# Gates of the last two layers: when they are stored, how their loads are buffered, and where their reciprocal stands

## The chip, the cores and the metric

The kernel runs on one core of a Trainium2 chip, as one launch. The time is what the device needs for one execution, in microseconds (us). Five engines run side by side, each through its own list of instructions in order: TensorE (PE) multiplies, VectorE (DVE), ScalarE (ACT) and GpSimd (POOL) do elementwise work, and SyncE (SP) here only issues transfers. An instruction that waits for a semaphore holds up all that stand behind it in the list of its engine; that holds for SP's list of transfers too.

## The reference, cut to what is computed

The model has two layers on x of 4 sequences with 512 tokens of 512 channels: a state-space block, a mixture of 8 experts (top 2), causal attention with 16 heads in 4 groups, and a gated feed-forward block. In front of each of the four blocks stands the same gate, computed from a second input f (used both as k and as v) and a condition:

```
def gate(r, k, v, w, u, time_emb):                # r = x, k = v = f
    tf = sigmoid(sum(time_emb, -1))
    decay = exp(-exp(w)) * (0.5 + 0.5 * tf)
    ek  = exp(minimum(k, 30));  ekv = ek * v
    nf, df = scan forward  of (a = a * decay + ekv, b = b * decay + ek)
    nb, db = scan backward of the same
    euk = exp(minimum(u + k, 30))
    num = nf + nb - ekv + euk * v
    den = df + db - ek + euk
    return sigmoid(r) * (num / maximum(den, 1e-8)) * (0.8 + 0.2 * tf)

x = x + mamba(gate0(x, f, f));  x = x + experts(gate1(x, f, f))
x = x + attention(gate2(x, f, f));  x = x + ffn(gate3(x, f, f))
```

All of the gate except sigmoid(r) depends on f and the condition alone, so it can be made long before x of its layer is known. ek and ekv are the same in all four layers.

## The kernel before

Everything is float32, in tiles of 128 partitions (channels) by 512 tokens. PE's work runs in stages: the state-space block, the experts, attention, the feed-forward block. The gates are made beside them, in the background.

**A pair.** `gate_pair(l, b, c0)` (L220) makes two 128-channel chunks of the gate of layer l and sequence b. It is a generator: its code is cut into steps by `yield True`, and inside a step `yield False` marks finer places to stop. In the text the steps are called S0 to S6:

- S0 `keys(0)`: on SP's list, the loads of f (tile `kt`, L239), of exp(k) (`ek`, L246) and of exp(k) k (`ekv`, L248) for the first chunk.
- S1: DVE's forward scan of the first chunk's numerator (L258, reads `ekv`), and `keys(1)`, the same three loads for the second chunk.
- S2: the backward scan (L264), then the forward scan of the second numerator.
- S3: its backward scan, and the forward scan of the first denominator (reads `ek`).
- S4: its backward scan, `own(0)` (three DVE operations, L275 to L279, that add the token's own term and read `kt`), the forward scan of the second denominator.
- S5: its backward scan, `own(1)`, and in the same step the reciprocal of both denominators on ACT (L315 and two more: relu, logarithm, exponential, each on 128x1024).
- S6: three DVE operations on 128x1024 (L321, L325, L330), and the store of the finished pair to `gts[l][b]` in HBM by SP (L332).

`kt`, `ek` and `num` have two buffers, everything else one. So the load of `ekv` for the second chunk, issued in S1, writes the buffer that S1's forward scan reads.

**The order.** `make_gates` (L341) strings the pairs together: the steps of one pair follow each other, S6 of a pair is done in the same step as S2 of the next one, and S0 of the next one in the same step as S5. A pair thus takes five steps. `pump(n)` (L371) runs n steps; `nudge` (L376) runs only to the next `yield` of either kind; `have(gate)` (L389) pumps until a gate is made.

**Layers 2 and 3** have 16 pairs, made from one generator during the experts and attention. During the experts, `more` (L1494) calls one `moe.round()` after another. A round of the experts is one block of 128 tokens: PE transposes and multiplies (`pg` L793, `pn` L804, `po` L826), and SP issues weight loads for a later block: two halves of w1 (L726, 1 MB each) with their bias (L731, 512 KB), w2 (L737, 1 MB) with its bias (L738). Two sets of weight tiles alternate between blocks, and each load carries a condition that leaves it out where the set already has the right expert. Behind each of 28 rounds stand one or two steps of the gates:

```
                moe.round()
                if moe.i < ALWAYS - NT + 1:
                    with after(nc.vector):
                        pump(1 + moe.i % 2)
```

`after` holds what is traced in it behind the last DVE instruction traced so far, on DVE alone; the places on SP's and ACT's lists are the scheduler's, which mostly keeps the order of the program. SP's list therefore holds, in turn, the weights of a round and the loads and the store of gate steps.

In attention, `scores` (L1598) calls `nudge` once for each of 4 query tiles of 64 heads, 256 times in all. The gate of layer 2 for sequence b+1 is asked for at the third head of sequence b in the first group (L1687), the gates of layer 3 in the feed-forward block.

Of the kernel before, what the change touches and what calls it, by code (L numbers as in the profile page):

```python
# [19 lines left out]
NC = C // P  # L20
# [62 lines left out]
def block_kernel(ctx: ExitStack, tc: tile.TileContext, a: dict, out: bass.AP):  # L83
    nc = tc.nc
# [129 lines left out]
    gts = [[dr.tile([P, NC, T], F32, name=f"g{l}_{b}") for b in range(B)] for l in range(4)]  # L214
# [5 lines left out]
    def gate_pair(l, b, c0, dst=None, tiles=None):  # L220


        many = {"kt": 2, "ek": 2, "num": 2}

        def tile_(tag, n=1):
            if tiles is not None and tag in tiles:
                return tiles[tag]()
            shape = [P, T] if n == 1 else [P, n, T]
            return gate_pool[0].tile(shape, F32, tag=tag, name=tag, bufs=many.get(tag, 1))

        flat = lambda t: t.rearrange("p i t -> p (i t)")
        d1 = [decay[:, l * NC + c0 + i, b : b + 1] for i in range(2)]
        fl = [fall[:, l * NC + c0 + i, b : b + 1] for i in range(2)]
        kt, ek, ekv, eu = {}, {}, {}, {}

        def keys(i):
            cc = c0 + i
            kt[i] = tile_("kt")
            nc.sync.dma_start(out=kt[i], in_=a["fT"][cc * P : (cc + 1) * P, b, :])  # L239
            ek[i] = tile_("ek")  # L240
            if l == 0:
                nc.vector.tensor_scalar(ek[i], kt[i], 30.0, None, ALU.min)
                act(ek[i], ek[i], AF.Exp)
                nc.sync.dma_start(out=eks[b][:, cc, :], in_=ek[i])
            else:
                nc.sync.dma_start(out=ek[i], in_=eks[b][:, cc, :])  # L246
                ekv[i] = tile_("ekv")
                nc.sync.dma_start(out=ekv[i], in_=ekvs[b][:, cc, :])  # L248

        def products(i):  # L250
            if l == 0:
                ekv[i] = tile_("ekv")
                nc.vector.tensor_tensor(ekv[i], ek[i], kt[i], ALU.mult)
                nc.sync.dma_start(out=ekvs[b][:, c0 + i, :], in_=ekv[i])


        def forward(i, e, s):
            nc.vector.tensor_tensor_scan(s, d1[i].to_broadcast([P, T]), e, 0.0, ALU.mult, ALU.add)  # L258
            f = tile_("f")
            nc.scalar.mul(f[:, : T - 1], s[:, : T - 1], fl[i])  # L260
            return f

        def backward(i, f, s):
            nc.vector.tensor_tensor_scan(  # L264
                s[:, : T - 1][:, ::-1], d1[i].to_broadcast([P, T - 1]), f[:, : T - 1][:, ::-1],
                s[:, T - 1 : T], ALU.mult, ALU.add,
            )

        def bonus(i):

            eu[i] = tile_("eu")
            act(eu[i], kt[i], AF.Exp, bias=col("wkv_u", l * NC + c0 + i))

        def own(i):
            nc.vector.scalar_tensor_tensor(den[:, i, :], eu[i], E30, den[:, i, :], ALU.min, ALU.add)  # L275
            yield False
            nc.vector.scalar_tensor_tensor(eu[i], eu[i], E30, kt[i], ALU.min, ALU.mult)
            yield False
            nc.vector.tensor_tensor(num[:, i, :], num[:, i, :], eu[i], ALU.add)  # L279
            yield False  # L280

        keys(0)
        yield True
        num = tile_("num", 2)
        products(0)
        f = forward(0, ekv[0], num[:, 0, :])
        keys(1)
        yield True
        backward(0, f, num[:, 0, :])
        yield False  # L290
        products(1)
        f = forward(1, ekv[1], num[:, 1, :])
        yield True
        backward(1, f, num[:, 1, :])
        yield False
        den = tile_("den", 2)
        f = forward(0, ek[0], den[:, 0, :])
        yield False
        bonus(0)
        yield True  # L300
        backward(0, f, den[:, 0, :])
        yield False
        yield from own(0)
        f = forward(1, ek[1], den[:, 1, :])
        yield False
        bonus(1)
        yield True
        backward(1, f, den[:, 1, :])
        yield False
        yield from own(1)  # L310
        if tiles is not None:
            yield True

        r = tile_("rec", 2)
        nc.scalar.activation(flat(r), flat(den), AF.Relu, bias=tiny[:, 1:2])  # L315
        yield False
        act(flat(r), flat(r), AF.Ln, bias=tiny[:, 0:1])
        yield False
        act(flat(r), flat(r), AF.Exp, scale=-1.0)
        yield True  # L320
        nc.vector.scalar_tensor_tensor(  # L321
            flat(den), flat(den), DEN_MIN, flat(r), ALU.max, ALU.mult
        )
        yield False
        nc.vector.scalar_tensor_tensor(  # L325
            flat(num), flat(num), tf_out[:, b : b + 1], flat(r), ALU.mult, ALU.mult
        )
        yield False
        g = num if dst is None else dst[:, c0 : c0 + 2, :]
        nc.vector.scalar_tensor_tensor(g, den, 2.0, num, ALU.subtract, ALU.mult)  # L330
        if dst is None:
            nc.sync.dma_start(out=gts[l][b][:, c0 : c0 + 2, :], in_=g)  # L332
        yield True

    def step(pair):
        for done in pair:
            if done:
                return
            yield False

    def make_gates(which):  # L341


        pairs = [(gate_pair(l, b, c0), (l, b), c0) for l, b in which for c0 in range(0, NC, 2)]
        yield from step(pairs[0][0])
        for n, (pair, _, _) in enumerate(pairs):
            yield True
            yield from step(pair)
            yield True
            yield from step(pair)  # L350
            if n:
                old, lb, c0 = pairs[n - 1]
                yield from step(old)
                made.update([lb] * (c0 + 2 == NC))
            yield True
            yield from step(pair)
            yield True
            yield from step(pair)
            yield True
            yield from step(pair)  # L360
            if n + 1 < len(pairs):
                yield from step(pairs[n + 1][0])
        yield True
        old, lb, c0 = pairs[-1]
        yield from step(old)
        made.add(lb)

    made = set()
    making = make_gates(((0, 1), (1, 0), (0, 2), (1, 1), (0, 3), (1, 2), (1, 3)))

    def pump(n=1, until=None):  # L371
        for _ in range(n):
            while until not in made and not next(making, True):
                pass

    def nudge():  # L376
        next(making, None)

    def apply_gate(g, xs):

# [8 lines left out]
    def have(gate):  # L389
        while gate not in made:  # L390
            pump()

    def gated(l, b, xb, pool, part=slice(0, T), **kw):
        have((l, b))
# [484 lines left out]
    with ExitStack() as ph:  # L879
# [41 lines left out]
        pairs = [gate_pair(0, 0, c0, first, lent[c0 // 2]) for c0 in range(0, NC, 2)]  # L921
# [388 lines left out]
        old = None  # L1310
# [178 lines left out]
    with tc.tile_pool(name="moe_w2", bufs=1, reuse_waits="tile") as wm:  # L1489
        moe.add_slot(wm)  # L1490
        for b in range(B):
            nc.sync.dma_start(out=x[b], in_=xs_d[b])

        def more(limit):  # L1494
            while moe.i < min(limit, moe.known):
                moe.round()
                if moe.i < ALWAYS - NT + 1:
                    with after(nc.vector):
                        pump(1 + moe.i % 2)

        more(moe.i + 1)
        next(routing)
        more(moe.i + 1)
        next(routing)
        more(moe.i + 1)
        order_blocks(NEARLY, NBLK)
        moe.know(ALWAYS)
        more(NBLK - 8)
        first_group = load_group(0)

        more(NEARLY + FIRST + 2)
        results = {t: load_results(0, t, nc.gpsimd) for t in range(2)}
        more(moe.i + 1)
        for t in range(NT):
            moe.round()
            with after(nc.tensor, nc.vector, nc.scalar):
                add_results(0, t, results.pop(t))
            if t + 2 < NT:
                results[t + 2] = load_results(0, t + 2, nc.gpsimd)
        assert moe.i == ALWAYS + 2  # L1520
        early_h = gated(2, 0, x[0], wa, tag="wq", name="h2_0")
        used = nc.values_load(in_use[0:1, 0:1], min_val=0, max_val=NBLK)
        with tc.If(used > ALWAYS - NEARLY):
            moe.i = ALWAYS
            moe.know(NBLK)
            for _ in range(4):
                moe.round()
# [5 lines left out]
    with att as ph:  # L1533
# [163 lines left out]
        dense(held[0])  # L1697
        for _ in making:
            pass
        act.use(act.SILU)  # L1700


# [113 lines left out]
```

## Time and profile before

| what | value |
|---|---|
| three runs, us | 2550.01, 2553.25, 2553.5 (median 2553.25) |
| the profiled execution: time, span, us | 2547.61, 2545.9 |
| busy share of the span: PE, DVE, ACT, POOL | 95%, 55%, 40%, 11% |
| mean granted TensorE clock | 0.984 |
| experts: first and last `pg` block, us from the start | 661.4 to 1125.7 |
| attention: first `pk` to last `pd`, us | 1143.6 to about 2085 |
| feed-forward block | about 2085 to the end |
| last gate store (L332), us | 1779.4 |

The profile is of one execution. Its own time is 1.71 us above its span, and 5.6 us under the median of the three runs. "Idle before" in a row of the profile is the time for which an engine had nothing to run just before the instructions of that row, and the arrow names what ended it.

### The profile page before, as it was taken

The numbers are of one execution on the slowest core, as the hardware profiler recorded it, in microseconds if no ns is written. First come the engines' busy times: TensorE is split into PE (matmuls) and PEld (weight loads), VectorE is DVE, ScalarE is ACT, GpSimd is POOL, SyncE is SP. The second block draws the span as 40 slices with busy tenths as digits, with TensorE's granted clock in tenths as the row PEclk, the third lists the DMA queues.
The fourth block names the chain that finished last, engine by engine and source line by source line (L and its number), as shares of the span: only waits on it lengthen the run. The fifth ranks groups of instructions, "written<-read, shape, count | busy, mean of one in ns | idle before, by whom it ended". The sixth has DMA issues, their size and how long they took to land.

```text
span 2545.9 us, 24316 instructions
## 1 busy us (share of the span) xinstructions
PE 2412.4 (95%) x8146; PEld 1283.8 (50%) x8146; DVE 1400.0 (55%) x2747; ACT 1008.1 (40%) x2050; POOL 279.3 (11%) x306
## 2 busy tenths in 40 slices
PE   3889999999998999999999999999999999999999
PEld 1544655556554444445555555555555544444444
DVE  8689999896346666745665555555344341010010
ACT  4576767667223334324454434444333331000000
POOL 4022423213311111110000000000000000000000
PEclk9889999999999999999999999999999999999999
DMA  6232523324254689765111101100000031000000
GB/s 216 68 107 71 186 76 133 125 83 167 78 178 145 238 288 358 260 222 196 58 45 38 50 30 33 63 25 9 1 17 17 17 115 38 17 4 13 8 9 17
DMA packets 86222, 243.04 MB, mean 95 GB/s; under 512 B 9424, under 2 KB 16976, under 8 KB 76880
## 3 DMA queue, kind: packets, MB, share of 16 engines
q1 hardware_dynamic: 77232, 215.78, 24.1%
q0 software_dynamic: 6560, 21.50, 2.5%
q10 hardware_dynamic: 2304, 4.20, 0.4%
q8 instruction: 65, 1.06, 0.2%
q14 instruction: 61, 0.50, 0.1%
HBM read 276.43 MB, written 46.53 MB: 127 GB/s over the span
## 4 chain that ended last, share of the span: by engine, by line
PE 49%; DVE 4%; ACT 2%; issue 0%; DMA 0%; ACTq 0%; SPq 0%
PE pd L1651 9%; PE pq L1587 7%; PE pfu L1725 6%; PE pfo L1735 6%; PE pfg L1720 6%; PE pctx L1636 5%; PE psc L1604 4%; PE pk L1565 2%; PE pv L1573 2%; PE ptp L1627 2%; DVE nmax L1609 1%; DVE psc L1607 0%; ACT pr L127 0%; DVE num L258 0%; DVE den L258 0%; DVE den L264 0%
## 5 line engine op out<-in xcount | busy, mean ns | idle before, releaser
L1587 PE MATMUL pq<-h,wq 128*128 128x512 f32 x512 | 245.3, 593 | 0.0
L1651 PE MATMUL pd<-cx,wd 128*128 128x512 f32 x512 | 222.4, 592 | 0.0
L1030 PE MATMUL pc<-h,wxb 128*128 128x512 f32 x320 | 147.5, 616 | 43.5 <-DVE h L1289 38.7
L1607 DVE TENSOR_TENSOR psc<-psc,mask 128x128 f32<-128x128 f32 x256 | 72.1, 287 | 206.8 <-PE psc L1604 205.7
L127 ACT ACTIVATE hd<-pfg,cols 128x512 f32<-128x512 f32 x44 | 30.2, 687 | 382.3 <-PE pfg L1720 382.3
L1730 DVE SCALAR_TENSOR_TENSOR hd<-pfu,cols,hd 128x512 f32<-128x512 f32 x44 | 33.0, 751 | 269.2 <-PE pfu L1725 269.1
L127 ACT ACTIVATE pr<-psc,nmax 128x128 f32<-128x128 f32 (+3 forms) x256 | 135.2, 529 | 92.2 <-DVE nmax L1609 91.7
L1725 PE MATMUL pfu<-h,ffu 128*128 128x512 f32 x352 | 158.7, 592 | 0.7 <-DMA ffu<-in_upT 0.7
L1720 PE MATMUL pfg<-h,ffg 128*128 128x512 f32 x352 | 158.8, 592 | 0.0
L1636 PE MATMUL pctx<-pT,v 128*128 128x512 f32 (+3 forms) x512 | 152.4, 441 | 3.9 <-ACT pT L1630 2.1
L793 PE MATMUL pg<-w,hT 128*128 128x512 f32 x296 | 139.1, 612 | 16.4 <-DMA w<-in_w1x 12.2
L1651 PEld LDWEIGHTS pd<-cx,wd 128*128 128x128 f32 x512 | 96.1, 190 | 114.8 <-issue 111.0
L1604 PE MATMUL psc<-kT,qT 128*128 128x128 f32 (+3 forms) x512 | 150.7, 434 | 1.6 <-ACT qT L1595 0.9
L1735 PE MATMUL pfo<-hd,ffd 128*128 128x512 f32 x352 | 151.7, 592 | 0.0
L1659 DVE TENSOR_TENSOR xr<-xr,pd 128x512 f32<-128x512 f32 x64 | 44.0, 687 | 190.9 <-PE pd L1651 190.9
L826 PE MATMUL po<-w,yT 128*128 128x512 f32 x296 | 136.4, 601 | 6.3 <-DMA w<-in_w2x 5.6
L1636 PEld LDWEIGHTS pctx<-pT,v 128*128 128x128 f32 x512 | 94.7, 191 | 92.9 <-issue 41.7
L804 PE MATMUL pn<-w,hT 128*128 128x512 f32 x296 | 133.4, 593 | 0.1
L1595 ACT ACTIVATE qT<-pq 128x512 f32<-128x512 f32 x64 | 38.2, 596 | 236.1 <-PE pq L1587 236.1
L1609 DVE TENSOR_REDUCE nmax<-psc 128x1 f32<-128x128 f32 (+3 forms) x256 | 123.8, 485 | 3.1
L1030 PEld LDWEIGHTS pc<-h,wxb 128*128 128x128 f32 x320 | 61.8, 198 | 115.4 <-issue 74.2
L1627 PEld LDWEIGHTS ptp<-ident,pr 128*128 128x128 f32 x640 | 77.6, 142 | 81.1 <-issue 39.4
(321 smaller groups left out, 4222.8 us busy)
## 6 DMA issues: line engine op xcount, KB each, us to landing
w<-in_w1x SPq DMA_DIRECT2D x76, 1024.0 KB
w<-in_w2x SPq DMA_DIRECT2D x38, 1024.0 KB
wb<-in_b1x SPq DMA_DIRECT2D x38, 512.0 KB
lm<-cs SPq DMA_DIRECT2D x32, 512.0 KB
kt<-in_fT SPq DMA_DIRECT2D x62, 256.0 KB
ek<-ek SPq DMA_DIRECT2D x62, 256.0 KB
ekv<-ekv SPq DMA_DIRECT2D x62, 256.0 KB
g<-num SPq DMA_DIRECT2D x30, 512.0 KB
```

Source lines behind the costliest of these rows:

```text
L127: nc.scalar.activation(*args, **kw)
L793: nc.tensor.matmul(pg, lhsT=hT[:, k, :], rhs=self.w1[s][0][:, k, :], start=(k == 0), stop=(k == NC - 1))
L826: nc.tensor.matmul(po, lhsT=yT[:, j, :], rhs=self.w2[s][:, j, :], start=(j == 0), stop=(j == NI - 1))
L1030: nc.tensor.matmul(pc, lhsT=wxb[:, k, m * P : (m + 1) * P], rhs=h[:, k, :], start=(k == 0), stop=(k == NC - 1),)
L1587: nc.tensor.matmul(pq, lhsT=u.wq[:, k, i * KVC : (i + 1) * KVC], rhs=u.h[:, k, :], start=(k == 0), stop=(k == NC - 1),)
L1604: nc.tensor.matmul(psc[:, :n], lhsT=qT[:, qi * P : n], rhs=u.kT[:, :n], start=True, stop=True)
L1609: nc.vector.tensor_reduce(nmax, psc[:, :n], AX.X, ALU.max, negate=True)
L1636: nc.tensor.matmul(pctx[:, kj * P :], lhsT=u.v[:, kj, :], rhs=pT[:, kj, kj * P :], start=(kj == 0), stop=(kj == NT - 1),)
L1651: nc.tensor.matmul(po, lhsT=u.wd[:, i, m * P : (m + 1) * P], rhs=u.ctxT[i], start=(i == 0), stop=(i == HPG - 1),)
L1720: nc.tensor.matmul(pg, lhsT=wg[:, k, cs], rhs=h[:, k, :], start=(k == 0), stop=(k == NC - 1))
L1725: nc.tensor.matmul(pu, lhsT=wu[:, k, cs], rhs=h[:, k, :], start=(k == 0), stop=(k == NC - 1))
L1735: nc.tensor.matmul(po, lhsT=wdn[:, i, m * P : (m + 1) * P], rhs=hd[i], start=(i == 0), stop=(i == NFF - 1),)
```

## The change

Three things are changed, all for layers 2 and 3 only. The tile `ekv` gets two buffers. `gate_pair` ends its step ahead of the reciprocal, and `make_gates` runs the reciprocal in a step of its own, which is also the one in which S0 of the next pair is run. S6 no longer issues its store: it is put into a list, and `send()` issues what is in the list. In the rounds of the experts `send()` stands behind the next round and ahead of its gate steps; `nudge` issues what was in the list before it ran; `have` and the end of attention issue the rest. For layers 0 and 1 the store is issued at once, as before.

```diff
-        many = {"kt": 2, "ek": 2, "num": 2}
+        many = {"kt": 2, "ek": 2, "num": 2, "ekv": 1 if l < 2 else 2}
...
         yield from own(1)
-        if tiles is not None:
+        if tiles is not None or l >= 2:
             yield True
         r = tile_("rec", 2)
...
         if dst is None:
-            nc.sync.dma_start(out=gts[l][b][:, c0 : c0 + 2, :], in_=g)
+            unsent.append((gts[l][b][:, c0 : c0 + 2, :], g))
+            if l < 2:
+                send()
         yield True
+
+    unsent = []
+
+    def send():
+        while unsent:
+            to, g = unsent.pop(0)
+            nc.sync.dma_start(out=to, in_=g)
...
             yield from step(pair)
+            if lb[0] >= 2:
+                yield True
+                yield from step(pair)
             if n + 1 < len(pairs):
                 yield from step(pairs[n + 1][0])
...
     def nudge():
+        old = list(unsent)
         next(making, None)
+        if old:
+            send()
...
     def have(gate):
         while gate not in made:
             pump()
+        send()
...
                     with after(nc.vector):
+                        send()
                         pump(1 + moe.i % 2)
...
         for _ in making:
             pass
+        send()
```

## The prediction, made before the changed kernel was run

> **What bounds the kernel now.** PE is busy for 95% of the span, so I looked for where it is not. On the page, two rows of the expert stage name transfers as what PE waited for:
>
> ```profile
> L793 PE MATMUL pg<-w,hT 128*128 128x512 f32 x296 | 139.1, 612 | 16.4 <-DMA w<-in_w1x 12.2
> L826 PE MATMUL po<-w,yT 128*128 128x512 f32 x296 | 136.4, 601 | 6.3 <-DMA w<-in_w2x 5.6
> ```
>
> See the last numbers: 12.2 + 5.6 = 17.8 us of PE idle until weights landed. The table of windows comes next (per stretch: its length, busy us of PE, PEld, DVE, ACT and POOL, then clock, DMA share, GB/s).
>
> ```profile
> 784.50:1122.70 338.20, 315.62 (x877) 147.94 (x876) 217.55 (x269) 121.78 (x167) 59.36 (x57) 0.98 0.73 266
> 880.60:944.50 63.90, 61.57 (x169) 28.85 (x168) 40.95 (x51) 25.21 (x33) 10.57 (x10) 0.97 0.90 324
> 1405.10:1750.80 345.70, 342.47 (x1249) 190.01 (x1249) 198.31 (x501) 151.13 (x379) 0.00 (x0) 1.00 0.11 36
> 1750.80:2032.60 281.80, 281.80 (x1044) 160.85 (x1043) 118.48 (x363) 98.78 (x273) 0.00 (x0) 1.00 0.04 14
> ```
>
> The first stretch is 27 rounds of the experts, 12.53 us each. An undisturbed round takes 11.17 (pg at 869.47 and 880.64). PE is idle for 22.6 us there. Attention has little to win: 3.2 us idle in 345.7.
>
> Why were the weights late? The waits of SP's own list, 800 to 1145 us (total, times, longest):
>
> ```profile
> SPq L332 <- DVE num L330: 37.9, 6, 12.9
> SPq L248 <- DVE num L258: 34.8, 8, 7.6
> SPq L737 <- PE po L826: 31.8, 10, 8.2
> SPq L239 <- DVE eu L277: 19.2, 3, 11.9
> ```
>
> The third is honest: w2 waits until its tile is free. The others are gate transfers waiting for DVE (the store for S6, the second `ekv` for S1's scan, `kt` for the own term), 91.9 us, and the next weights stand behind them. The timeline shows it at the longest stall, SP first, then PE:
>
> ```profile
> 813.92 0.07 SPq L731 DMA_DIRECT2D wb<-in_b1x  x1
> 821.57 0.34 SPq L332 DMA_DIRECT2D g<-num  x1
> 822.32 0.34 SPq L726 DMA_DIRECT2D w<-in_w1x  x1
> 824.37 0.34 SPq L726 DMA_DIRECT2D w<-in_w1x  x1
> ```
>
> ```profile
> 820.74 3.60 PE L804 MATMUL pn<-w,hT 128*128 128x512 f32 x8
> 829.59 6.50 PE L793 MATMUL pg<-w,hT 128*128 128x512 f32 x8 [5.25 <-DMA w<-in_w1x]
> ```
>
> SP stood 7.6 us at the store, the weights went out at 822.32, and PE, done with pn at 824.34, waited 5.25 us. Then eight matmuls took 6.50 us instead of 3.60.
>
> **What the change takes away.** I traced each weight stall on PE back to what held SP:
>
> - 829.59: 5.25 idle + 2.90 slow clock (6.50 - 3.60). The store.
> - 857.09 and 862.05: 2.09 + 0.85. `kt` held to 848.00, `ekv` to 853.62.
> - 913.50: 2.25, and ten matmuls in 6.25 us where 4.46 is usual (3.60 + 2 x 0.43), so 1.79. `ekv` to 895.55, the store to 901.88.
> - 957.03 and 969.47: 0.61 + 1.02. The store, from 936.6 to 949.67.
> - 990.17 and 996.59: 1.54 + 2.75. `ekv`, from 973.9 to 982.40.
> - 1053.22: 0.51, `kt`; 1107.44: 0.97, `ekv`.
>
> Idle 17.84 + slow clock 4.69 = 22.5 us. A store sent after the next round meets an S6 that ran about a round (11 us) earlier. The second `ekv` buffer is last read in the pair before, so its wait goes wholly. `kt` of S0 is last read in S4; with the extra step between, S4 is always in an earlier round. What is late next is the honest wait for free tiles, and the wire. I take 80%: **18.0 us**. Ends: 8.15 (the store stall of 829.59 alone) and 22.5.
>
> The clock term deserves a weighing. The Trainium skill (TensorE: Matmul & The Clock Gate, Part 1) says that PE falls to half clock after an idle window of about 3.4 us and regains full clock after as much busy time. By the rule, only the 5.25 us stall counts, for half of 3.4 = 1.7; the one of 2.25 us costs nothing. The sum would be 17.84 + 1.7 = 19.5, and 80% of it 15.6. The rows show 2.90 and 1.79. I use the rows.
>
> A rule against the change: DMA: Bandwidth & Descriptors (Specifications) puts HBM at about 358 GB/s for a core; an earlier issue makes no bandwidth. The row 880.60:944.50 runs at 324 GB/s with engines 90% busy. By the rule its 63.9 x 324 = 20.7 MB need 57.8 us, below the 61.57 that PE is busy there; for all 27 rounds, 338.2 x 266 = 90 MB need 251 us against 27 x 11.17 = 302. So on average the wire leaves room, though little in that stretch (933.30:944.50 even moved 379 GB/s, over the rule's figure). This is why I keep 20% back.
>
> **The reciprocal.** In the experts ACT waits for the own term at L315 8 times, 27.5 us (ACT's waits, 750 to 1145). Once it hurt PE: the block began at 793.03, ran to 799.0 (three operations of 1.15, 1.15, 1.06 us and two table loads of 1.28), the copy of `hT` stood behind it, and pg at 800.02 lost 4.18 idle + 1.80 slow clock (5.40 - 3.60) = 6.0. In its own step the reciprocal finds its sums done, but its 5.8 us stay, and where ACT's list puts `hT` is not known. Ends 0 and 6.0; I take half, since one of eight hurt: **3.0**.
>
> **What it adds.** One step per pair. The 28 rounds run 42 steps: before, 8 x 5 + 2, which finishes 7 pairs; after, 7 x 6, which finishes 6. Counting the yields (21 per pair before, 22 after), 169 nudges finish the gates in attention before and 203 after, 34 more. A group of 4 heads (16 nudges) takes 345.7 / 6 = 57.62 us with gates beside it and 281.8 / 5 = 56.36 without: 1.26 / 16 = 0.079 us per nudge, times 34 = **2.7 us** lost. Upper end: the three groups from 1222.60 to 1405.10 take 60.83 each, 4.47 over the bare one, or 9.5 us for 34, though the results of the experts are added there too. The lower end is 0. By date nothing is missed: gate (2,3) is made at nudge 30 and asked for after 40; the last at 203 of 256, some 120 us later than now, still ahead of the feed-forward block.
>
> Six steps are four rounds exactly, so S4 + S5 always share a round. DVE needed 8.4 us for them (786.04 to 794.4) and 5 x 0.69 = 3.45 for the round: 11.85 against PE's 11.17. The neighbours have one scan pair or nothing, and PE wants the result only in the next round: 0, at most 7 x 0.68 = 4.8. The second buffer costs 2 KB per partition and shifts later tiles; no row prices it, no instruction is added: 0, bounded by a microsecond of shifted waits either way. No transfer is added; 16 stores move behind a round's weights on SP, and the only reader near (gate (2,0) at 1123.77) needs pairs stored long before.
>
> **Sum.** -18.0 - 3.0 + 2.7 = -18.3 us, on the profiled 2547.6: 2529.3. The runs' median is 5.6 above that execution, so 2553.25 - 18.3 = **2535**. About 0.2% (5.1 us) is what a measurement of this kernel can tell from no change.
>
> **The rivals.**
>
> - *The wire takes SP's place* (14%). For: 90% busy engines at 880 to 945, 82% to 1008. The stalls in those stretches (913.50 to 996.59: 8.17 idle + 1.79) stay. Against: before 957 and 990 SP was blocked for 13 and 8 us and then caught up with two rounds' loads at once, which spreads when SP is free. Gain 22.5 - 10.0 - 2.7 = 9.8: 2543.5.
> - *It doesn't do what it says* (11%): the scheduler sets the store elsewhere on SP's list, or SP stands just as long at the next wait (`w2` for PE, 31.8 us). For: SP's order is not written out by hand. Against: at 821.57 to 824.37 it follows the program. Gain about what attention costs: 2550 to 2556.
> - *Slower* (11%): the gate work pushed into attention costs the upper price, at 1143 to 1405 where DVE and ACT also add the expert results. For: PE idles there already, 3.00 us at 1187.73. Against: one nudge still runs one piece, no more per head than now. It decides where the experts give back less than those 9.5 us; with 2.7 given back, 2560.
> - The forecast itself: 64%, its own range 2525 (all 28.5 regained, attention costing nothing) to 2545 (half of 22.5 regained, nothing from ACT).
>
> The range 2523 to 2554 takes in the forecast with its microsecond or two of shifted waits, the wire and half of "no change", and leaves out about 0.17. Chances: faster 0.64 + 0.14 = 0.78, same 0.11, slower 0.11.
>
> **What would show it.** In the changed profile SP's waits at L332 for S6 and L248 for the scan are gone from the expert stage, and L239's is small; PE's wait for w1 falls from 12.2 to under 3 us, w2's from 5.6 to under 2; pg at about 829 starts without idle; PEclk in 784 to 841 rises from 0.91; attention begins 18 to 24 us earlier; the last gate store comes some 34 nudges later against the start of attention. I am wrong if the same weights are late with SP free (the wire), if pg waits for `hT` after each reciprocal, or if groups in attention take over 58 us up to the last store.

## The result, and the profile after

The changed kernel takes 2543.16 us (median of 20 runs, 2535.04 to 2554.14) against 2555.24 for the kernel before (20 runs, 2547.03 to 2560.89). The ratio is 0.9959, with a 95% interval of 0.9948 to 0.9971: about 10.5 us faster by the ratio (the two medians lie 12.1 apart), a little over half of the 18.3 that were forecast, and inside the range. The profiled execution took 2543.18 us with a span of 2541.5.

The two rows of the page that answer to those shown before (line numbers have moved by 17):

```profile
L810 PE MATMUL pg<-w,hT 128*128 128x512 f32 x296 | 137.1, 605 | 7.2 <-ACT hT L783 6.8
L843 PE MATMUL po<-w,yT 128*128 128x512 f32 x296 | 135.9, 600 | 6.2 <-ACT yT L836 6.2
```

Weights are no longer named: of 17.8 us of PE's waits for them 0.3 are left. In their place stands ACT, with 6.8 + 6.2 us (12.8 of them in the expert stage as it is counted below) for two copies, `hT` and `yT`, that turn a PE result into the next operand. SP's own waits, 800 to 1145 us (total, times, longest), show why the weights are on time:

```profile
SPq L754 <- PE po L843: 87.3, 27, 10.1
SPq L743 <- PE pn L821: 41.1, 21, 3.8
SPq L755 <- DVE o L848: 36.4, 22, 3.9
SPq L743 <- PE pg L810: 20.5, 10, 7.7
```

Not one of these is a gate transfer. SP now waits for tiles to come free, that is for PE, and is ready when they do. The timeline of SP where the long stall was (about 6 us later here, see below):

```profile
827.77 0.09 SPq L754 DMA_DIRECT2D w<-in_w2x  x1
828.50 0.08 SPq L755 DMA_DIRECT2D wb<-in_b2x  x1
831.65 0.34 SPq L743 DMA_DIRECT2D w<-in_w1x  x1
832.39 0.34 SPq L748 DMA_DIRECT2D wb<-in_b1x  x1
832.78 0.43 SPq L343 DMA_DIRECT2D g<-num  x1
```

The store stands behind the weights of its round and goes out at once: the DVE operation that makes it had ended at 827.77. What ACT does to PE is seen in its timeline; here at the worst place, first ACT, then PE:

```profile
798.07 0.72 ACT L123 ACTIVATE eu<-kt,cols 128x512 f32<-128x512 f32 x1 [2.30 <-DVE num L279]
799.55 1.15 ACT L315 ACTIVATE rec<-den,tiny 128x1024 f32<-128x1024 f32 x1 [0.76 <-DVE den L275]
800.71 1.28 ACT L123 ACT_TABLE_LOAD   x1
802.01 1.15 ACT L123 ACTIVATE rec<-rec,tiny 128x1024 f32<-128x1024 f32 x1
803.17 1.28 ACT L123 ACT_TABLE_LOAD   x1
804.47 1.06 ACT L123 ACTIVATE rec<-rec 128x1024 f32<-128x1024 f32 x1
805.43 0.58 ACT L836 ACTIVATE yT<-pyt 128x512 f32<-128x512 f32 x1
805.91 0.58 ACT L783 COPY hT<-pfl 128x512 f32<-128x512 f32 x1
```

```profile
806.54 6.15 PE L810 MATMUL pg<-w,hT 128*128 128x512 f32 x8 [4.17 <-ACT hT L783]
```

The reciprocal has a step of its own, and still starts the moment DVE has made its sums ("0.76 <-DVE den L275"): nothing holds it back on ACT's list. For 5.9 us the two copies wait behind it, PE waits for `hT`, and then runs eight matmuls in 6.15 us instead of 3.60. The one such wait before, and the second worst after, are these:

```profile
800.02 5.40 PE L793 MATMUL pg<-w,hT 128*128 128x512 f32 x8 [4.18 <-ACT hT L766]
```

```profile
951.41 5.40 PE L843 MATMUL po<-w,yT 128*128 128x512 f32 x8 [3.28 <-ACT yT L836]
```

Before, one of the eight reciprocals in the experts held PE up. Now all six do: those that begin at 799.55, 851.16 and 899.01 cost PE 4.17, 1.32 and 1.33 us for `hT`, those at 945.32, 995.26 and 1041.57 cost 3.28, 1.33 and 1.34 us for `yT`.

By stage, in the profiled executions: from the second list of expert blocks (the last `pidx<-of` matmul) to the first `pk` block the experts take 368.3 us before and 355.8 after; from there to the start of the last `pd` block, attention takes 929.7 and 930.9; the rest 472.6 and 472.9. That is -12.5 + 1.2 + 0.3 = -11.0 us, between the 10.5 of the ratio and the 12.1 of the medians. The spans differ by only 4.4, because the stage ahead of the experts took 775.3 us in the one profile and 781.9 in the other. Its instructions are the same in both kernels, in the same order on each engine, but for one wait of SP that the second `ekv` buffer takes away. Over all the profiles of this study that stage lies between 775.3 and 788.2, and behind_only below, a kernel that leaves all but the end of that stage as it was before, has one of the longest (788.0). So it is taken for chance of the execution, and the stages are compared and not the spans.

### The profile page after: what moved, and what is told of

The parts are those of the page before. It is cut to its first block, busy times and chain, and to the rows that moved or that the text cites. A ratio compares the mean times of both kernels' runs of the same rounds, so it can differ in the third digit from the quotient of the medians.

```text
span 2541.5 us, 24336 instructions
## 1 busy us (share of the span) xinstructions
PE 2412.8 (95%) x8146; PEld 1286.5 (51%) x8146; DVE 1405.3 (55%) x2760; ACT 1002.1 (39%) x2035; POOL 278.6 (11%) x306
## 4 chain that ended last, share of the span: by engine, by line
PE 48%; DVE 4%; ACT 3%; DMA 0%; issue 0%; SPq 0%; ACTq 0%
PE pd L1669 9%; PE pq L1605 7%; PE pfu L1744 6%; PE pfo L1754 6%; PE pfg L1739 6%; PE pctx L1654 5%; PE psc L1622 3%; PE pv L1591 2%; PE pk L1583 2%; PE ptp L1645 2%; DVE nmax L1627 1%; DVE num L258 1%; ACT pr L127 1%; DVE psc L1625 0%; DVE num L264 0%; ACT pT L1648 0%
```

## The experiments

The theory after the result: the queue part of the forecast was right and even too small, and the missing 8 us went to the reciprocal, whose place on ACT's list the change left open. The rivals: attention pays more than was counted; the weights are still bound somewhere; the own step is harmful in itself.

The table gathers what the profiles show. Waits of PE are those in the experts, in us: for weights, and for the chain of `hT`, `yT` and `u` (`u` is DVE's product that is turned into `yT`). The ratio is to the kernel before, run in the same set. The changed kernel was not run again in the later sets, so where the text gives a time against it, that is a difference of medians of two sets; by the ratios the distance is 13 us instead of 9.3 for no_split, 6 instead of 7.4 for store_now, 23 instead of 18.4 for act_behind.

| kernel | waits: weights | waits: hT, yT, u | experts | attention | ratio, 95% interval |
|---|---|---|---|---|---|
| before | 17.8 | 4.7 | 368.3 | 929.7 | 1 |
| changed | 0.3 | 13.5 | 355.8 | 930.9 | 0.9959 (0.9948 to 0.9971) |
| no_split | 3.5 | 6.1 | 350.6 | 927.4 | 0.9907 (0.9883 to 0.9931) |
| store_now | 7.5 | 8.8 | 359.8 | 932.6 | 0.9982 (0.9970 to 0.9994) |
| ekv_one | 0 | 13.5 | 355.8 | 931.2 | 0.9944 (0.9921 to 0.9967) |
| act_behind | 0 | 1.0 | 337.5 | 932.8 | 0.9870 (0.9843 to 0.9897) |
| no_split_behind | 2.3 | 6.1 | 347.3 | 927.4 | 0.9925 (0.9897 to 0.9952) |
| two_steps | 6.7 | 19.2 | 371.8 | 924.3 | 1.0038 (1.0025 to 1.0052) |
| behind_only | 16.9 | 4.8 | 368.7 | 930.2 | 1.0006 (0.9990 to 1.0022) |
| split_only | 7.6 | 8.8 | 361.5 | 931.9 | 0.9970 (0.9958 to 0.9983) |
| hold_relu | 0 | 1.0 | 337.1 | 932.9 | 0.9884 (0.9868 to 0.9900) |
| late_only | 6.8 | 6.6 | 354.3 | 930.0 | 0.9940 (0.9928 to 0.9953) |
| ekv_only | 12.4 | 5.2 | 361.9 | 930.2 | 0.9961 (0.9947 to 0.9974) |

### no_split: the changed kernel without the reciprocal's own step

```diff
-        if tiles is not None or l >= 2:
+        if tiles is not None:
             yield True
...
-            if lb[0] >= 2:
-                yield True
-                yield from step(pair)
```

> The changed kernel, but with the reciprocal back in the step of own(1): the late store and the two ekv buffers alone, five steps for a pair. Theory A (the reciprocal's own step is what costs: six steps are four rounds, so the block of 5.9 us always meets the copies yT and hT at the same bad place): PE's waits for hT and yT in the expert stage fall from 12.8 us to under 6, weights stay under 2, and the time is 4 to 9 us below the changed kernel, some 16 to 20 below before. Theory B (with the weights on time any reciprocal block shows, wherever its step stands, since before it hid behind late weights): the waits for hT and yT stay at 10 to 18 us and the time is within 3 us of the changed kernel. The kt waits on SP should come back, 10 to 20 us in all, and cost PE under 3 us.

2533.85 us, 9.3 below the changed kernel. ACT waits fall to 4.2 + 1.9, about the 6 of theory A, and both stages gain: 5.2 us in the experts, 3.5 in attention. So theory A is right on this pair of kernels: the own step, as the change has it, costs more than it brings. SP waits 36.2 us at `kt` again, more than expected, and weights are 3.5 us late instead of under 2: one stall at 856.47, behind a wait at `kt` of 1.93 us that ended at 845.93 and three gate loads behind it. That the whole stall comes from there is not shown.

### store_now: the changed kernel with the store in the step that makes it

```diff
             unsent.append((gts[l][b][:, c0 : c0 + 2, :], g))
-            if l < 2:
-                send()
+            send()
```

> The changed kernel, but each finished pair is stored at once in the step that makes it. If the late store was the larger half of the gain (15.6 of the 22.5 us of stalls were put down to stores, alone or with ekv), SP waits for DVE at the store again, some 30 us in all, PE waits for w1 or w2 by 4 to 8 us, and the time is 4 to 9 us above the changed kernel. If the other two edits alone free SP enough, PE's waits for weights stay under 2 us and the time is within 3 us of the changed kernel.

2550.6 us, 7.4 above the changed kernel. The waits of SP and of PE that came back, between 775 and 1150 us:

```profile
SPq L342 <- DVE num L330: 46.5, 6, 10.1
```

```profile
PE pg L809 <- ACT hT L782: 8.8, 3, 4.2
PE pg L809 <- DMA w<-in_w1x: 7.5, 2, 4.1
```

Of 46.5 us at the store on SP 7.5 reach PE, two stalls of some 4 us, as forecast for the larger half.

### ekv_one: the changed kernel with one ekv buffer

```diff
-        many = {"kt": 2, "ek": 2, "num": 2, "ekv": 1 if l < 2 else 2}
+        many = {"kt": 2, "ek": 2, "num": 2, "ekv": 1}
```

> The changed kernel, but with one buffer for ekv. SP waits at the second ekv load for the scan again, 25 to 40 us in all in the expert stage. If that wait costs weights, PE waits for w1 or w2 by 3 to 8 us and the time is 3 to 8 us above the changed kernel; if the loads have room because the store no longer stands behind it, PE waits under 2 us and the time is within 3 us.

SP waits 35.1 us for the scan again, and no weight is late: experts 355.8 us, as in the changed kernel, and the intervals of the two ratios overlap. Beside a late store and the own step, the second buffer is worth nothing that can be measured.

### act_behind: the changed kernel with the gate steps held on ACT too

```diff
-                    with after(nc.vector):
+                    with after(nc.vector, nc.scalar):
                         send()
                         pump(1 + moe.i % 2)
```

> The changed kernel, with one word more: in the rounds of the experts the gate steps are held behind the last ACT instruction traced too, which is the copy of hT for the next block, not only behind the last DVE instruction. If the remaining loss is the place of the reciprocal on ACT's list, PE's waits for hT and yT fall from 12.8 us to under 3, the clock in the expert stage rises to 0.99, and the time is 10 to 17 us below the changed kernel. If the block of 5.9 us is too long for any place in a round of 11.2 us, the waits only move to yT or to DVE and the time stays within 4 us of the changed kernel.

2524.81 us, 18.4 below the changed kernel (17 at most were expected) and 13 in a thousand below the one before: faster than both. The same place as above, ACT and then PE:

```profile
795.07 0.58 ACT L836 ACTIVATE yT<-pyt 128x512 f32<-128x512 f32 x1
795.55 0.57 ACT L783 COPY hT<-pfl 128x512 f32<-128x512 f32 x1
796.01 1.16 ACT L315 ACTIVATE rec<-den,tiny 128x1024 f32<-128x1024 f32 x1
797.19 1.28 ACT L123 ACT_TABLE_LOAD   x1
798.48 1.15 ACT L123 ACTIVATE rec<-rec,tiny 128x1024 f32<-128x1024 f32 x1
```

```profile
798.57 3.60 PE L810 MATMUL pg<-w,hT 128*128 128x512 f32 x8
803.17 0.63 PE L834 MATMUL pyt<-ident,u 128*128 128x128 f32 x4 [1.00 <-DVE u L828]
```

The same block starts behind `hT` instead of ahead of it. `pg` starts without idle, and what is left of the harm is 1.00 us, because `u` hangs on a tanh that ACT did late. The windows of the experts (length, busy PE, PEld, DVE, ACT, POOL, clock, DMA share, GB/s), of the kernel before, of the changed one, and of act_behind:

```profile
775.33:1143.63 368.30, 341.28 (x958) 160.38 (x959) 230.16 (x293) 130.20 (x181) 66.55 (x66) 0.98 0.71 259
```

```profile
781.85:1137.67 355.82, 337.52 (x958) 160.16 (x959) 212.79 (x275) 115.58 (x164) 65.25 (x66) 0.98 0.74 262
```

```profile
778.22:1115.68 337.46, 331.99 (x959) 159.11 (x959) 212.30 (x275) 114.86 (x164) 63.96 (x65) 1.00 0.77 276
```

PE's idle time (length less busy) goes from 27.0 us to 18.3 to 5.5, and its busy time for the same 958 matmuls from 341.3 to 337.5 to 332.0, because the clock is not lost any more. The stage moves its bytes (276 GB/s x 337 us = 93 MB, 95 before) in 31 us less than before; the DMA engines are then busy for 77%.

### no_split_behind and two_steps: is the own step needed, and is there room for more gates?

no_split_behind is no_split with the hold of act_behind; two_steps is that with

```diff
-                        pump(1 + moe.i % 2)
+                        pump(2)
```

> The late store and two ekv buffers, five steps for a pair, and the gate steps held behind the copy of hT on ACT. If the two gains add (no own step was worth 5.2 us in the experts and 3.5 in attention, the place on ACT 18.3 us in the experts), the ACT waits of PE in the experts are under 3 us, that stage takes 333 to 342 us and attention 926 to 930, and the time is 2 to 7 us below act_behind. If the own step was only bad for where it set the reciprocal on ACT, the experts take as long as in act_behind (337.5) and only attention's 3 us remain. If the kt wait that comes back (36.2 us on SP in no_split) now costs weights, PE waits over 4 us for w1 or w2 and the time is above act_behind.

Neither of the three. Without its own step the reciprocal gains almost nothing from being held: ACT waits stay at 4.2 + 1.9 us, and the experts take 347.3 us, 3.3 less than in no_split and 9.8 more than in act_behind. So the own step is not harmful in itself. With the hold it is worth 9.8 us in the experts, less 5.4 in attention; without it, it costs 5.2 and 3.5. With the own step the experts also contain six reciprocals instead of eight, because a pair takes more steps; how much of the 9.8 us is owed to that was not separated.

> As no_split_behind, with two gate steps behind every round of the experts in place of one and two in turn: 56 steps, 10 pairs made there in place of 7, and 59 nudges of 169 fewer in attention. At 0.08 to 0.1 us for a nudge attention takes 921 to 925 us. If DVE (7.1 us of gates and 3.5 of its own in a round of 11.2) and the wire still have room, the experts keep to within 3 us of no_split_behind and the time is 2 to 7 us below it. If DVE or the DMA engines become the bound there, PE waits for DVE or weights by more than 8 us, and the time is above it.

Attention gains as expected (924.3 us). The experts lose 24.5 us against no_split_behind, and the kernel is slower than before. Three of PE's waits there:

```profile
PE po L840 <- ACT yT L833: 12.2, 6, 3.4
PE pg L807 <- DMA w<-in_w1x: 6.7, 4, 3.6
PE pyt L831 <- DVE u L825: 2.8, 1, 2.8
```

No engine is full on average (DVE 251.8 us of 325 between 785 and 1110), yet everything is late at once. SP stands 73.3 us at `kt`: S0 and S4, the load and the last reader of its buffer, can share a round wherever a pair has five steps, and the wait comes 14 times here against 6 in no_split_behind.

### behind_only and split_only: one part alone, on the kernel before

behind_only changes `with after(nc.vector):` as act_behind does; split_only takes over the own step and nothing else.

> The kernel before, with nothing but the gate steps of the expert rounds held behind the copy of hT on ACT. If the place on ACT was a small loss there (one stall of 4.2 us and 1.8 of slow clock) and late weights the large one, PE's waits for weights stay at 12 to 20 us, the experts take 361 to 368 us (368.3 before) and the time is 0 to 7 us below before. If late weights only took the blame for the reciprocal, the experts fall under 355 us.

No change (ratio 1.0006), experts 368.7 us where 361 to 368 were expected, weights 16.9 us late. The order on ACT was worth nothing while weights were late: its one stall of 4.2 us stays too. There the reciprocal shares its step with `own(1)`, so that it has to wait for DVE wherever it is held; that this is why the hold does nothing is argued, not shown.

> The kernel before, with nothing but the reciprocal's own step. The kt wait on SP (23.3 us) should fall under 5. If stores and ekv are what makes weights late and the own step costs, PE waits 10 to 18 us for weights and 6 to 14 for hT and yT, the experts take 366 to 378 us, attention about 3 us more than before, and the time is 1 to 12 us above before. If freeing kt is worth more than the rest, the experts fall under 362 us.

The second of the two outcomes, by a little: 0.9970, experts 361.5 us (under 362). SP's wait at `kt` is gone, and the store waits 19.3 us instead of 37.9, so weights are 7.6 us late, below the 10 that were expected; ACT waits rise from 4.7 to 8.8 us as expected. The own step thus also leaves SP a shorter wait for S6, which may be because it spreads the work; which of the two waits brings more was not separated.

### hold_relu: the hold on the reciprocal alone

```diff
-        nc.scalar.activation(flat(r), flat(den), AF.Relu, bias=tiny[:, 1:2])
+        with after(*[nc.scalar] * (l >= 2)):
+            nc.scalar.activation(flat(r), flat(den), AF.Relu, bias=tiny[:, 1:2])
```

> The changed kernel, with the first operation of the reciprocal alone, in layers 2 and 3, held behind the last ACT instruction traced (in the expert rounds the copy of hT), and nothing else moved. If the place of that one block on ACT's list is the whole of what act_behind gave, PE's waits for hT and yT in the experts are under 3 us, the experts take 335 to 341 us (355.8 in the changed kernel, 337.5 in act_behind), and the time is within 3 us of act_behind. If act_behind gained by holding the other gate work on ACT, the waits stay over 8 us and the experts over 348.

2526.62 us; experts 337.1, ACT waits 1.0. It is act_behind to within 2 us, from one held instruction per pair. The place of that block is, as far as these runs can tell, the whole of what act_behind gave.

### late_only and ekv_only: the two other parts alone

late_only is no_split with one `ekv` buffer; ekv_only is the kernel before with two.

> The kernel before, with the late store alone. SP's waits for DVE at the store should go (37.9 us), those at ekv (34.8) and kt (23.3) stay or grow. If the store was the larger part of the late weights, PE's waits for weights fall from 17.8 to 6 to 12 us, the experts take 354 to 362 us (368.3 before) and the time is 6 to 14 us below before. If SP only stands as long at the next gate load, weights stay over 14 us late and the experts over 363.

> The kernel before, with the second ekv buffer alone. SP's waits for the scan at ekv should go (34.8 us). If they are the smaller part of the late weights, PE's waits for weights fall from 17.8 to 10 to 15 us, the experts take 360 to 366 us and the time is 2 to 8 us below before. If SP only stands as long at the store behind it, weights stay over 15 us late and the experts over 366.

Waits and stages are as expected: weights 6.8 and 12.4 us late instead of 17.8, experts 354.3 and 361.9. The times fell a little further than the ranges allowed: by 14.1 us (14 at most) and 8.6 us (8 at most) in the medians, with ratios of 0.9940 and 0.9961. In ekv_only SP stands longer at the store (54.6 us, 37.9 before), so part of the wait only moved.

## Why the prediction was right, and where its sum was off

- **The weights (-18.0 forecast).** Right, and too cautious. The waits fell by 17.5 us, and the 4.69 us of slow clock behind them went too: 22.2 us, close to the upper end of 22.5. The fifth kept back for the wire (the moving of the bytes itself) was not needed. Put in one after another, the late store takes 11.0 us off the waits (late_only), the second buffer 3.3 more (no_split), the own step the last 3.2 (changed). But the order matters: with store and own step in place the buffer takes nothing (ekv_one).
- **The reciprocal (-3.0 forecast).** This is the term that failed, in its sign. I held that "in its own step the reciprocal finds its sums done" and that at worst nothing is gained (ends 0 and 6.0). The changed profile has the waits for `hT`, `yT` and `u` at 13.5 us and slow clock behind two of them, (6.15 - 3.60) + (5.40 - 3.60) = 4.35, together 17.9, against 4.7 + 1.8 = 6.5 before: +11.4. What was overlooked is that a step decides when an instruction is traced, not its place on a list that nothing binds: ACT still took the reciprocal as soon as the sums were there (six waits for L275, 3.6 us in all), and where that was ahead of the copies, PE waited. The forecast had named the place of `hT` on ACT's list as unknown and still put the loss at nothing; its own sign of being wrong, that `pg` waits for `hT` after each reciprocal, came true for three of six, and `po` waits for `yT` after the other three. act_behind and hold_relu show that the place is the cause: the same step, held, gives 18.3 and 18.7 us in the experts. Why all six blocks hit here is open. That six steps make four rounds, so that the block comes back at about the same point, does not settle it: in store_now and split_only it does so too, and three of six hit.
- **The sum of the experts.** -22.2 + 11.4 = -10.8; measured -12.5. The idle part agrees (27.0 - 18.3 = 8.7, and 17.5 less, 8.8 more). PE's busy time fell by 3.8, where the slow groups listed account for 2.1: the 1.7 between lie there and were not traced further.
- **Attention (+2.7).** Right within its ends. Six steps against five, with all else equal, cost 3.5 us (930.9 and 927.4), 5.4 with the hold. Against the kernel before only 1.2 show, since no_split is 2.3 below it there. These lie ahead of the first `pd` block (78.8 us from the first `pk` before, 76.2 in no_split); what makes them is open. The last gate store stands at 1890.4 us, 111 later than before, where some 120 had been worked out.
- **DVE's heavy rounds (0) and the shifted tiles (0).** Nothing shows. The one wait of PE for DVE, 0.7 us for `u`, is ACT's again: DVE itself stood 3.46 us for a tanh that ACT did behind a reciprocal.
- **The rivals.** The wire took no one's place: act_behind moves more per us than before (276 against 259 GB/s) and waits for no weight, as the forecast's average had it. The store's place on SP's list is the one traced. The upper price of attention was not paid.
- **The start of attention (18 to 24 us earlier forecast).** It came 6.0 us earlier (1143.6 and 1137.7), 12.5 when the longer stage ahead is taken off.
- **The hit itself.** That the total fell into the range is in part luck. The reciprocal's +11.4 lies outside its own ends (-6.0 to 0). With the other terms as forecast it would have made 2553.25 - 18.0 + 11.4 + 2.7 = 2549.4, which the range holds only because it had been widened for the wire and for half of "no change", neither of which happened. That the weights gave 4.2 us more than forecast, and attention took less, made up for a part of it. The measured 2543.16 is almost the 2543.5 of the wire rival, which had no part in it.

## What to carry to other kernels

On a list that runs in order, a transfer that waits for compute is a wait for all behind it, so send background stores a round late and look first at which queue stands still, not at how busy the wire is. When one wait is removed, list the next one on every engine of the same loop. Late weights had not merely hidden it here: with the weights nearly on time and no own step (no_split) PE waits 6.1 us for ACT, 4.7 before, and 13.5 with the own step; half of the gain went back to the step that was to free ACT. Whether a step of its own helps background work depends on the place that it is given on each engine it touches: without a hold on ACT it brought 6.8 us in the experts to the kernel before and took 5.2 from the one with the late store; with it, one held instruction per pair was worth 18.7 us.

## What the hardware did that was not expected

PE lost clock after idle stretches shorter than I had thought. Groups of eight matmuls that need 3.60 us took 3.67 after 2.09 us of idle and 3.70 after 1.33, but 5.40 after 3.28 and 6.15 after 4.17, and 2.25 us of idle was once followed by ten in 6.25 (4.46 usual), while 2.75 us cost nothing (3.67, at 996.59 before). The rule of the Trainium skill (TensorE: Matmul & The Clock Gate, Part 1) of about 3.4 us would have let the 2.25 and the 3.28 go free.

The length of one idle stretch alone does not decide it. The record of the granted clock shows what does. In the profile before, the stretches at half clock in the experts and at the start of attention begin at 801.15, 828.45, 913.79 and 1142.48 us, which are 8, 25 and 67 times 3.413 us apart, and they last 3.41 or 6.83 us. Cut along this grid, the two cases look like this (length, busy PE, clock; the last two columns, DMA, do not matter here):

```profile
910.38:913.79 3.41, 1.16 (x4) 1.00 1.02 414
913.79:917.20 3.41, 3.41 (x5) 0.50 1.01 420
992.33:995.74 3.41, 1.51 (x4) 1.00 1.00 417
995.74:999.15 3.41, 2.56 (x6) 1.00 1.02 423
```

The 2.25 us fall into one step of the grid and leave PE idle in 2.25 of its 3.41 us; the next step runs at half clock. The 2.75 us are divided between two steps, with idle of 1.90 and 0.85, and nothing follows. From the start of the experts to that of attention the 13 profiles of this study have 104 steps, each cut along its own profile's grid, that ran at full clock with more than 0.8 us of PE idle. Of those with more than 2.05 us idle 39 of 39 are followed by half clock, of those from 1.85 to 2.05 us 3 of 8, of those with less none of 57. So in these kernels a stall costs clock where it leaves PE idle for some 2 us or more of one step.

The stage ahead of the experts, in all but its end the same instructions in the same order, differed by up to 12.9 us between profiled executions (775.3 to 788.2 us). That is about the whole effect of this change, and single spans would have hidden it.
